# A two-layer graph kernel: the stage between its layers takes its rows in source order and shares PSUM with the second layer

## The chip, the cores and the metric

One core of a Trainium2 chip. The metric is the time of one execution on the device in microseconds (us). The engines are TensorE (PE; its weight loads are listed as PEld), VectorE (DVE), ScalarE (ACT), GpSimd (POOL) and SyncE (SP, which here only issues DMA transfers). SBUF is the on-chip memory of 128 partitions. PSUM is the matrix engine's output memory; the kernel allots it in eight banks of 2 KB a partition, each of which holds one 128 x 512 tile of f32.

## The reference

`x` is 4096 x 512, `adj` is 4096 x 4096, all f32. `adj` has about 1.6% entries that are not zero, and the whole diagonal. Layer 0 is attention with one head whose logits get the matrix added twice; layer 1 has eight heads of 64.

```
# layer 0
h = relu(layernorm(x))
q, k, v = h @ Wq.T + bq, h @ Wk.T + bk, h @ Wv.T + bv
x = x + softmax(q @ k.T * scale + adj + adj) @ v
# layer 1
h   = relu(layernorm(x))
nX  = (h @ W) as heads, (8, 4096, 64)
nX  = a_ln * (nX - mean) / (std(nX, ddof=1) + 1e-6) + b_ln
at1, at2 = nX . a1, nX . a2                      # per head and row
kg  = leaky_relu(at1 + at2.T, 0.2) * adj
att = softmax(where(adj != 0, kg, -32768))
out = x + elu(att @ nX + nX)
```

## The kernel before

**Names.** N = 4096 rows, D = 512. A block is 128 rows (P), NB = 32 of them; a chunk is SB = 4 blocks, 512 rows (GC), NI = NS = 8 of them. R = 32. HD = 64 is a head, HG = 4 heads make a head group. `seq(...)` keeps an engine's instructions in the order in which the program issues them, DMA queues included; so the order of the Python calls is the order on each engine, and instructions of different engines are held together by semaphores alone.

**Layer 0** (the loop at L742) goes over 8 chunks of 512 query rows by 32 tiles of 128 keys, two tiles at a time. PE makes logits (L585) and weighted values (L636), both as seven products for eight. At a chunk's end `chunk_end` (L671) puts the products M1 to M7 together on DVE and ACT (`ends`, L694), `total_of_rows` (L710) sums the softmax totals on PE, `divide` (L680) scales four blocks on ACT and adds `x` by an accumulating DMA from POOL's queue, and `normalize_rows` (L271) makes the layernorm of the new rows and stores it to `xn_d`, and the new rows to `x1_d`. Along the way `for_layer_1` stores the transposed matrix for layer 1: `gT_d` in f32 and a mask `nT_d` in bf16. The pool `early` holds the tiles that read the matrix (`ag`). The last chunk's `ends`, totals and divide come after the loop.

**Source order.** In layer 1 a tile of 128 sources takes rows p = 32q + r from block q of a chunk, so that tile c of a chunk has partition 32q + r hold row 128q + 32c + r. In layer 0 and in the stage before the change a block is 128 rows in their own order; `rows_of_sources` (L106) and `sources_of_rows` (L110) are views that change from one order to the other in a DMA.

**The stage between the layers** (L1073 to L1273) is a loop over blocks r. `load_normalized` loads a chunk of `xn_d` (1 MB) to `xns`. `turn(r)` transposes a block on PE (four 128 x 128) and takes relu on ACT. `project(r)` is 16 products 128 x 264 with the centred weights, to `y` in PSUM (two banks), the last 16 columns being the head sums with a1 and a2. `variance(r)` is a square on ACT, a sum by heads on DVE, and a maximum and a power -1/2 on POOL. `standardize(r)` refines the root in five small DVE operations, multiplies `y` by it to `feat` (which sets y free) and to `at`, and POOL multiplies a_ln to `own`. Once a chunk, `split` makes on DVE (14 operations) the three bf16 pieces of at1 and at2; `sides` turns them on PE for each block, copies on ACT and stores to `z1_d` and `z2_d`; `fours` does the same for `u4_d`. `store_features` writes `feat` to `nX_d`, `store_rows` writes `own` to `own_d`, and `load_targets` brings -4 times at2 (stored to `at2_d`) back in source order. `at_block(r, f)` puts a step behind block r; what is left after the loop runs in the first steps of layer 1 (`at_step`, `later`). PSUM has its own pool here: `turned` 1 bank, `y` three times 2, `side` 1. It is closed before layer 1 opens one of the same size.

**Layer 1** (from L1285) is 512 steps (8 chunks of target rows by 2 head groups by 32 source tiles); 32 steps make a group. In a step PE forms the logits of four heads (`left_sums` L888 for the next step, `sums` L878 and L908), ACT and DVE take relu and leaky, DVE and POOL multiply by the matrix `g` (L935, L932), ACT takes exp (L939), and PE multiplies by the features `nX` (L951) of four steps before, in accumulators that live for a group. Every four steps `load_adj` issues `z2`, `nb`, two `nx` and `g` (1 MB) on SP, and in the first group `load_features` issues four loads of 256 KB of `nX_d`, which go to `nX` in SBUF, in source order, for the rest of the kernel. `finish` ends a group: `copies` of the two accumulators by ACT and DVE, `to_rows` transposes on PE, `divide`, own_d added by POOL's queue (step +5), `negative` (+8), `positive`, exp, a sum (+12), x1_d added (+15), and `close` (+21) writes out.

```
        for r in range(-1, NB + 1):
            if r + 1 < NB:
                turn(r + 1)
            if 0 <= r < NB:
                project(r)
            if r >= 1:
                standardize(r - 1)
            if 0 <= r < NB:
                variance(r)
            for f in at_blocks.pop(r, []):
                f()
```

Of the kernel before, what the change touches and what calls it, by code (L numbers as in the profile page):

```python
# [79 lines left out]
def fast_path(  # L80
# [64 lines left out]
    x1_d = dram.tile([NI, 2, P, 2, SB, P], F32, name="x1_d")  # L145
# [10 lines left out]
    nX_d = dram.tile([NB, P, D], F32, name="nX_d")  # L156
    own_d = dram.tile([NI, 2, P, 2, SB, P], F32, name="own_d")
    u4_d = dram.tile([NB, NH, P], F32, name="u4_d")
    at2_d = dram.tile([NB, P, NH], F32, name="at2_d")

    def store_rows(ap, ic, rows, n):
        seq(nc.sync.dma_start(out=ap[ic, n // 2, :, n % 2], in_=rows[:, :, ts(n, P)]))
# [147 lines left out]
    with tc.tile_pool(name="early", bufs=2) as early, tc.tile_pool(name="kv", bufs=1) as kv:  # L310
# [17 lines left out]
        def load_adj0(s):  # L328

            ic, jt = TILES[s]  # L330
            ag = early.tile([P, GC // R, P], F32, name="ag", tag="ag", bufs=2)
            load_blocks(ag, adj[ts(ic, GC), ts(jt // SB, GC)])
            for c in range(SB):
                raws[s + c] = ag
# [44 lines left out]
        with tc.tile_pool(name="proj_c", bufs=1) as pc, tc.tile_pool(  # L379
# [10 lines left out]
            def load_x(sb):  # L390
                xt = early.tile([P, SB, D], F32, name="xt", tag="ag", bufs=2)
                for b in range(SB):
                    seq(nc.sync.dma_start(out=xt[:, b, :], in_=x[ts(sb * SB + b, P), :]))
                return xt
# [154 lines left out]
        with tc.tile_pool(name="attn", bufs=2) as work, tc.tile_pool(  # L549
# [121 lines left out]
            def chunk_end(s, ic):  # L671
# [19 lines left out]
                def then(*pairs):  # L691
                    return lambda: [seq(f(*a)) for f, *a in pairs]

                ends.extend([  # L694
                    then((copy, c11, m[1])),
# [14 lines left out]
            def total_of_rows(ic):  # L710
# [9 lines left out]
                rows_of[ic] = work.tile([P, SB], F32, name="rinv", tag="rinv", bufs=2)  # L720
# [21 lines left out]
            for s in range(0, n_tiles, 2):  # L742
# [31 lines left out]
                if jt == 0 and ic:  # L774
                    total_of_rows(ic - 1)
                weighted(s, (3, 0), (3, 1), (6, 0), (6, 1))
# [12 lines left out]
            total_of_rows(NI - 1)  # L789
            while ends:  # L790
                end()
            rests[0]()
# [5 lines left out]
    with tc.tile_pool(name="ga_g", bufs=2) as adjs, tc.tile_pool(  # L798
# [3 lines left out]
    ) as work, ExitStack() as banks:  # L802
        psum = banks.enter_context(tc.tile_pool(name="stage_ps", bufs=2, space=PSUM))
# [60 lines left out]
        def pair_rows(ap, ic, hg):  # L864

            r, c = cols(ic, hg)
            return [
                ap[r, c.start + f * P : c.start + (f + 1) * P].rearrange("(b p) d -> p b d", p=P)
                for f in range(2)
            ]  # L870
# [70 lines left out]
        def values(n, hf):  # L941
# [3 lines left out]
            if jt == 0 and hf == 0:  # L945
                grp["acc"] = [
                    psum.tile([P, GC], F32, name=f"acc{hf}", tag=f"acc{hf}", bufs=1) for hf in range(2)
                ]
            t = logits.pop(n) if hf else logits[n]
            for e in range(2):  # L950
                seq(nc.tensor.matmul(  # L951
                    grp["acc"][hf][ts(e, HD), :], nX[jt // SB][:, jt % SB, hg * HG + 2 * hf + e, :],
                    t[:, hf + 2 * e, :], start=jt == 0, stop=jt == NB - 1,
                ))

        def finish(n, ic, hg):
# [3 lines left out]
            y = work.tile([P, 2, SB * 2, HD], F32, name="y", tag="y", bufs=1)  # L960

            def room():
                grp["e"] = work.tile([P, 2, SB * 2, HD], F32, name="e", tag="ob", bufs=1)

            def copies():
                seq(nc.scalar.copy(ob[:, 0, :], grp["acc"][0]))
                seq(nc.vector.tensor_copy(ob[:, 1, :], grp["acc"][1]))

            def to_rows(hf, ks=range(2)):
# [12 lines left out]
                grp["pt"] = pt[:, :, 0 : 4 * HB].rearrange("p k (q c) -> p k q c", c=HB)  # L982

            def divide(hf, ks=range(2)):
                v = grp.pop("pt")
                rinv = inverses[:, ic, hg, hf, ks[0] : ks[-1] + 1]
                seq(nc.vector.reciprocal(rinv, v[:, :, :, HD]))  # L987
                seq(nc.vector.tensor_mul(  # L988
                    y[:, hf].rearrange("p (k q) e -> p k q e", k=2)[:, ks[0] : ks[-1] + 1],
                    v[:, :, :, 0:HD],  # L990
                    rinv.unsqueeze(3).to_broadcast([P, len(ks), 4, HD]),
                ))

            def add(t, what):
                seq(nc.gpsimd.dma_start(out=flat(t), in_=what, accum_op=ALU.add))

            def of_group(ap):
                return ap[ic, hg].rearrange("p f b d -> p (f b d)")

            def flat(t):  # L1000
                return t.rearrange("p f q e -> p (f q e)")
# [10 lines left out]
            def close():  # L1012
                e = grp["e"]
                for f, ap in enumerate(pair_rows(out, ic, hg)):
                    nc.sync.dma_start(
                        out=ap, in_=e[:, f].rearrange("p (b h) e -> p b (h e)", h=2)
                    )

            if n > n_steps:

                of_rows = [last_in[0][:, 2 * k : 2 * k + 2, :] for k in range(2)]

                def half(t, hf):
                    return t[:, hf].rearrange("p q e -> p (q e)")
# [8 lines left out]
                for hf in range(2):  # L1033
                    seq(nc.vector.tensor_add(half(y, hf), half(y, hf), of_rows[0][:, hf]))
# [3 lines left out]
                for hf, queue in enumerate((nc.sync, nc.scalar)):  # L1038
                    seq(nc.vector.tensor_add(half(e, hf), half(e, hf), half(y, hf)))
                    seq(nc.vector.tensor_add(half(e, hf), half(e, hf), of_rows[1][:, hf]))  # L1040
                    queue.dma_start(
                        out=pair_rows(out, ic, hg)[hf],
                        in_=e[:, hf].rearrange("p (b h) e -> p b (h e)", h=2),
                    )
# [6 lines left out]
            for d, f in (  # L1051
                (5, lambda: add(y, of_group(own_d))), (8, room), (8, negative), (9, positive),
                (10, lambda: exp_of(flat(grp["e"]))), (12, lambda: add(grp["e"], flat(y))),
                (15, lambda: add(grp["e"], of_group(x1_d))), (21, close),
# [3 lines left out]

        def load_features(k):
            nX.append(gat.tile([P, SB, NH, HD], F32, name=f"nX{k}"))  # L1060
            for q in range(SB):
                seq(nc.sync.dma_start(
                    out=nX[k][q * R : (q + 1) * R].rearrange("p c h e -> p c (h e)"),
                    in_=nX_d[k * SB + q].rearrange("(c r) d -> r c d", r=R),
                ))
# [10 lines left out]
        xns, feats, owns, states, ys, deviating = {}, {}, {}, {}, {}, {}  # L1076
# [6 lines left out]
        def load_normalized(ic):  # L1083
# [4 lines left out]
            seq(nc.sync.dma_start(out=xns[ic], in_=by_blocks(xn_d, ic)))  # L1088

        def turn(r):  # L1090
            m = psum.tile([P, GC], F32, name="turned", tag="turned", bufs=1)
# [4 lines left out]
        def project(r):  # L1096
            ys[r] = psum.tile([P, 2, GC], F32, name="y", tag="y", bufs=3)
            for g in range(2):
                for k in range(KC):
                    seq(nc.tensor.matmul(  # L1100
                        ys[r][:, g, 0:HW], h1s[:, r % 2, ts(k, P)], w1_sb[:, k, g, :],
                        start=k == 0, stop=k == KC - 1,
                    ))
# [14 lines left out]
        def standardize(r):  # L1118
# [9 lines left out]
            if b == 0:  # L1128
                feats[ic], owns[ic] = chunk_tile("feat"), chunk_tile("own")
                states[ic] = prep.tile([P, SB, 2, NH], F32, name="at", tag="at", bufs=2)  # L1130
            f, o = feats[ic][:, b, :], owns[ic][:, b, :]
# [16 lines left out]
        def split(ic):  # L1148

            at = states.pop(ic)  # L1150
            seq(nc.vector.tensor_add(
                at, at, at_b.unsqueeze(1).to_broadcast([P, SB, 2, NH])
            ))
            at2s = prep.tile([P, SB, NH], F32, name="at2s", tag="at2s", bufs=2)
            seq(nc.vector.tensor_scalar_mul(at2s, at[:, :, 1, :], -4.0))
            rows = slice(ic * SB, (ic + 1) * SB)
            def store_targets():
                seq(nc.sync.dma_start(out=at2_d[rows].rearrange("q p h -> p q h"), in_=at2s))

            if ic + 1 < NI:  # L1160
                at_block(SB * ic + 5, store_targets)
            else:
                at_step(2, store_targets)
            at1s = prep.tile([P, SB, NH], F32, name="at1s", tag="at1s", bufs=2)
            seq(nc.vector.tensor_scalar_mul(at1s, at[:, :, 0, :], 4.0))
            at2c = prep.tile([P, SB, NH], F32, name="at2c", tag="at2c", bufs=1)
            seq(nc.vector.tensor_mul(
                at2c, at[:, :, 1, :], coef.rearrange("p b g f e -> p b (g f e)")
            ))
            for e, (kind, first) in enumerate(((2, 3), (0, 0))):  # L1170
                rest = prep.tile([P, SB, NH], F32, name="rest", tag="rest", bufs=2)
                left = at2c if e else at[:, :, 0, :]
                for i in range(3):
                    piece = parts[:, :, kind : kind + 2, :, first + i]
                    seq(nc.vector.tensor_copy(piece, left.rearrange("p b (g h) -> p b g h", h=HG)))
                    if i < 2:
                        seq(nc.vector.tensor_sub(
                            rest.rearrange("p b (g h) -> p b g h", h=HG),
                            left.rearrange("p b (g h) -> p b g h", h=HG), piece,
                        ))  # L1180
                        left = rest
            at1ss[ic] = at1s

        def one_bank(tag):
            return banks_now[0].tile([P, GC], F32, name="m", tag=tag, bufs=1)

        banks_now = [psum]

        def sides(ic, b, tag="side"):
# [573 lines left out]
```

## Time and profile before

| what | value |
| --- | --- |
| median of three runs (lowest, highest) | 3669.55 us (3669.5, 3675.35) |
| the profiled execution: its own time, its span | 3669.51 us, 3667.7 us |
| mean granted clock of PE | 0.988 |
| busy: PE, DVE, ACT, POOL | 97%, 69%, 48%, 62% |
| first transpose of the stage (L1093) | 1846.28 us |
| first product of layer 1 (L888) | 2029.72 us |
| first group of layer 1 ends, 32 steps later | 2151.94 us |
| a step of layer 1 in its steady part | 2.968 us |

The span is the time from the first to the last instruction; 1.8 us of the execution lie around it. The rows that follow further down come from these views: the page's 40 slices (a digit is the busy share of a slice of 91.7 us in tenths); the waits (engine, line, what was waited for, total us, times, the longest); the timeline (start, length, engine, line, operation, tiles with their shapes, count, and in brackets the idle time ahead with what ended it); windows (length, then busy time and instructions of PE, PEld, DVE, ACT and POOL, the granted clock, the DMA engines' share, GB/s); and the chain of waits (start, length, what the end of the kernel depended on then).

### The profile page before, as it was taken

To read this page: it belongs to the slowest core of one execution; us is meant where nothing else is said; L and a number is where in the kernel's file an instruction comes from. 1 tells how busy PE (TensorE), PEld (TensorE's weight loads), DVE (VectorE), ACT (ScalarE), POOL (GpSimd) and SP (SyncE) were. 2 spreads that over 40 slices of the span, in tenths; PEclk is the share of its full clock that TensorE was granted. 3 is DMA by queue.
4 is the path that set the end of the run, shared out by engine and by line. 5 is a ranking of instruction groups with operands and counts; after the bars stand their busy time and mean duration, and the time that the engine had idled before them with its cause. 6 is when DMAs were issued, how large, how long until landed. Compare 5 with 4: busy or idle time off the path is not lost. (4 is left out here: it accounts for less than half of the span.)

```text
span 3667.7 us, 58811 instructions
## 1 busy us (share of the span) xinstructions
PE 3546.0 (97%) x21482; PEld 2085.7 (57%) x21482; DVE 2536.0 (69%) x4163; ACT 1746.5 (48%) x1541; POOL 2269.8 (62%) x1802
## 2 busy tenths in 40 slices
PE   8999999999999999999988789999999999999998
PEld 4447888888888888888866223222222222222232
DVE  5435565656566666656555678888888888888887
ACT  1000011111111111111133679999999899999997
POOL 4653444444444444444455568788887787888886
PEclk9999999999999999999999899999999999999999
DMA  6566788888888787888658987788877777777875
GB/s 213 181 210 207 234 240 246 231 247 242 244 235 243 242 249 243 229 256 235 199 146 212 220 206 208 205 216 212 215 205 207 197 200 210 206 211 216 210 210 151
DMA packets 667531, 796.85 MB, mean 217 GB/s; under 512 B 86817, under 2 KB 489697, under 8 KB 658017
## 3 DMA queue, kind: packets, MB, share of 16 engines
q1 hardware_dynamic: 655136, 759.64, 71.7%
q0 software_dynamic: 10704, 31.98, 5.0%
q8 instruction: 171, 2.80, 0.3%
q10 hardware_dynamic: 1392, 1.38, 0.2%
q14 instruction: 128, 1.04, 0.1%
HBM read 602.28 MB, written 182.71 MB: 214 GB/s over the span
## 5 line engine op out<-in xcount | busy, mean ns | idle before, releaser
L932 POOL TENSOR_TENSOR t<-t,g 128x1024 f32<-128x1024 f32 x512 | 1223.8, 2402 | 316.8 <-DVE t L926 226.7
L951 PE MATMUL acc<-t,nX 128*64 128x512 f32 x4096 | 1009.1, 609 | 0.0
L939 ACT ACTIVATE t<-t 128x2048 f32<-128x2048 f32 (+1 forms) x527 | 976.6, 1853 | 0.2 <-POOL t L932 0.2
L926 DVE SCALAR_TENSOR_TENSOR t<-u,at2m,r 128x512 f32<-128x512 f32 x1024 | 719.2, 744 | 205.6 <-issue 150.0
L597 ACT ACTIVATE aT<-aT 128x512 f32<-128x512 f32 x256 | 161.2, 630 | 1405.5 <-DVE aT L593 1405.5
L593 DVE TENSOR_TENSOR aT<-aT,XZ 128x256 f32<-128x256 f32 x893 | 352.3, 418 | 584.9 <-PE XZ L585 580.3
L935 DVE TENSOR_TENSOR t<-l,g 128x1024 f32<-128x1024 f32 x512 | 623.4, 1218 | 27.8 <-DMA g<-gT_d 24.7
L894 ACT ACTIVATE l<-l 128x1024 f32<-128x1024 f32 x512 | 516.4, 1009 | 155.4 <-PE l L888 108.2
L951 PEld LDWEIGHTS acc<-t,nX 128*64 128x64 f32 x4096 | 247.7, 136 | 456.7 <-issue 448.9
L585 PE MATMUL XZ<-qt,hS 128*128 128x256 f32 x2040 | 483.8, 380 | 1.9 <-DVE aT L593 1.0
L585 PEld LDWEIGHTS XZ<-qt,hS 128*128 128x128 f32 x2040 | 387.5, 190 | 57.8 <-DVE aT L593 5.1
L609 POOL TENSOR_TENSOR S<-aT 128x256 f32<-128x256 f32 x128 | 93.2, 728 | 519.8 <-ACT aT L597 519.8
L585 PE MATMUL XZ<-qt,hT 128*128 128x256 f32 x1532 | 372.5, 379 | 0.5 <-DVE aT L593 0.5
L621 POOL TENSOR_TENSOR total<-total,aT 128x256 f32<-128x256 f32 x360 | 323.2, 911 | 9.4
L585 PEld LDWEIGHTS XZ<-qt,hT 128*128 128x128 f32 x1532 | 291.0, 190 | 40.4 <-DVE aT L593 0.9
L878 PEld LDWEIGHTS <-z 6*128 6x128 bf16 x2048 | 52.3, 91 | 428.3 <-DVE t L926 344.8
L610 POOL TENSOR_TENSOR aT<-aT 128x256 f32<-128x256 f32 x128 | 93.2, 728 | 285.4 <-ACT aT L597 285.4
L636 PE MATMUL M<-v,aT 128*128 128x256 f32 x1024 | 262.8, 379 | 0.0
L636 PE MATMUL M<-tv,aT 128*128 128x256 f32 x1024 | 262.6, 379 | 0.0
L636 PE MATMUL M<-v,S 128*128 128x256 f32 x1024 | 242.5, 380 | 0.0
L888 PE MATMUL l<-z_left,z 64*64 64x512 bf16 x2048 | 203.1, 383 | 34.4 <-DVE t L935 20.9
L577 DVE SCALAR_TENSOR_TENSOR gs<-ng,aT 128x512 f32<-128x512 bf16 x256 | 225.8, 882 | 8.8
(188 smaller groups left out, 4383.8 us busy)
## 6 DMA issues: line engine op xcount, KB each, us to landing
g<-gT_d SPq DMA_DIRECT2D x128, 1024.0 KB
ag<-in_adj_dram SPq DMA_DIRECT2D x256, 256.0 KB
hS<-s_d SPq DMA_DIRECT2D x64, 1024.0 KB
gT_d<-gs SPq DMA_DIRECT2D x256, 256.0 KB
nb<-nT_d SPq DMA_DIRECT2D x128, 512.0 KB
nx<-nT_d SPq DMA_DIRECT2D x256, 256.0 KB
hT<-h_d SPq DMA_DIRECT2D x64, 768.0 KB
tv<-vt_d SPq DMA_DIRECT2D x128, 384.0 KB
```

What stands on the lines that cost most here:

```text
L577: seq(nc.vector.scalar_tensor_tensor(gs, ng, G_MASKED / NEG_BIG, aT, ALU.mult, ALU.add))
L585: seq(nc.tensor.matmul(out, a, b, start=start and k == 0, stop=k == 1, skip_group_check=not start,))
L593: seq(nc.vector.tensor_add(p, p, part))
L621: seq(nc.gpsimd.tensor_add(t, t, a))
L636: seq(nc.tensor.matmul(sums[ic][i][:, u, :], a[:, ts(u, P)], b, start=jt == 0 and u == 0, stop=jt == NB - 2, skip_group_check=u == 1,))
L888: seq(nc.tensor.matmul(lefts[n][ts(c, HD), r, :], loads[n // JB][2][ts(r, HD), jt % JB * P + c * HD :][:, :HD], groups[ic, hg]["z1_left"][ ...
L894: seq(nc.scalar.activation(lefts[n], lefts[n], AF.Relu, scale=4.0))
L926: seq(nc.vector.scalar_tensor_tensor(t[:, 2 + e, :], u4[:, e, :], at2m[:, jt, h : h + 1], right[e], ALU.max, ALU.add))
L932: seq(nc.gpsimd.tensor_mul(t[:, 2:4, :], t[:, 2:4, :], both_heads(n)))
L935: seq(nc.vector.tensor_mul(logits[n][:, 0:2, :], lefts.pop(n), both_heads(n)))
L939: seq(nc.scalar.activation(t, t, AF.Exp))
L951: seq(nc.tensor.matmul(grp["acc"][hf][ts(e, HD), :], nX[jt // SB][:, jt % SB, hg * HG + 2 * hf + e, :], t[:, hf + 2 * e, :], start=jt == 0 ...
```

## The change

1. `load_normalized` loads each chunk as four transfers of 32 partitions, in source order. `standardize` then writes the features at once to `nX` in SBUF, and `split` writes `at2m`. `nX_d`, `at2_d` and their stores and loads are gone. The stores of `z1_d`, `z2_d`, `u4_d` and `own` change order on the way (`own_d` by four transfers of 32 partitions a chunk). `ones_in` stands in the stage.
2. `variance(r)` is issued ahead of `standardize(r - 1)`.
3. One PSUM pool serves the stage and layer 1. The accumulators are one tile `accs` of two banks, for the whole pool; `y` is that tile for every third block and an `l` tile otherwise; `turn` uses r0 (the first r1), `sides` and `fours` r1.
4. `split` stays behind block 4 of the next chunk; `sides` and `fours` come two to three blocks later, some of them inside a projection. Those of the last chunk, its split in eight parts of two operations, and the last `standardize`, stand in layer 1's first 18 steps.
5. At the end of layer 0 the last chunk's additions are grouped anew (two copies on ACT), the totals stand before the last eight products, the divide comes after block 0, and the `ag` tiles have a pool of their own, so that `xns` can be loaded before layer 0 has ended.
6. `x1_d`, `own_d`, `y` and `e` have another layout: `close` is one transfer with runs of 1 KB instead of two with runs of 512 B; the addition of own_d has runs of 1 KB for 4 KB.

```diff
-    x1_d = dram.tile([NI, 2, P, 2, SB, P], F32, name="x1_d")
+    x1_d = dram.tile([NI, 2, P, SB, 2, P], F32, name="x1_d")
...
+                ] if ic + 1 == NI else [
...
+                if not more:
+                    end()
+                    total_of_rows(ic)
                 weighted(s, (3, 0), (3, 1), (6, 0), (6, 1))
...
-            total_of_rows(NI - 1)
-            while ends:
-                end()
-            rests[0]()
...
-        psum = banks.enter_context(tc.tile_pool(name="stage_ps", bufs=2, space=PSUM))
+        accs = psum.tile([P, 2, GC], F32, name="accs", tag="accs", bufs=1)
...
-                seq(nc.scalar.copy(ob[:, 0, :], grp["acc"][0]))
-                seq(nc.vector.tensor_copy(ob[:, 1, :], grp["acc"][1]))
+                seq(nc.scalar.copy(ob[:, 0, :], accs[:, 0, :]))
+                seq(nc.vector.tensor_copy(ob[:, 1, :], accs[:, 1, :]))
...
-                for f, ap in enumerate(pair_rows(out, ic, hg)):
-                    nc.sync.dma_start(
-                        out=ap, in_=e[:, f].rearrange("p (b h) e -> p b (h e)", h=2)
-                    )
+                nc.sync.dma_start(
+                    out=rows_out(ic, hg), in_=grp["e"].rearrange("p b f h e -> p b (f h e)")
+                )
...
-            seq(nc.sync.dma_start(out=xns[ic], in_=by_blocks(xn_d, ic)))
+            for q in range(SB):
+                seq(nc.sync.dma_start(
+                    out=xns[ic][ts(q, R)],
+                    in_=xn_d[ic * SB + q].rearrange("(c r) d -> r c d", r=R),
+                ))
...
-            m = psum.tile([P, GC], F32, name="turned", tag="turned", bufs=1)
+            m = one_bank("r0" if r else "r1")
...
-            ys[r] = psum.tile([P, 2, GC], F32, name="y", tag="y", bufs=3)
+            if r % 3 == 1:
+                ys[r] = accs
+            else:
+                ys[r] = psum.tile([P, 2, GC], F32, name="y", tag="l", bufs=2)
...
-            f, o = feats[ic][:, b, :], owns[ic][:, b, :]
+            f, o = nX[ic][:, b].rearrange("p h e -> p (h e)"), owns[ic][:, b, :]
...
+        def store_own(ic, q):
+            seq(nc.sync.dma_start(
+                out=own_d[ic].rearrange("(c r) b g f d -> b r c (g f d)", r=R)[q],
+                in_=owns[ic][ts(q, R)],
+            ))
...
+            places = (k + 6, k + 7, (k + 8, 3), k + 8) if ic + 2 < NI else (
+                k + 6, (k + 7, 2), (k + 7, 5), k + 7)
...
+        for ic in range(NI - 1):
+            at_block(SB * ic + 4, split_all, ic)
...
-        for r in range(-1, NB + 1):
+        for r in range(-1, NB):
             if r + 1 < NB:
                 turn(r + 1)
-            if 0 <= r < NB:
+            if r >= 0:
                 project(r)
+                variance(r)
             if r >= 1:
                 standardize(r - 1)
-            if 0 <= r < NB:
-                variance(r)
...
+        later[0, "mid"] = [lambda: standardize(NB - 1)]
...
+        def split_last():
+            pieces = split(NI - 1)
+            for n in range(2, 10):
+                later.setdefault((n, "end"), []).append(lambda: some_of(pieces, 2))
...
-            if n % JB == (2 if q == NS - 1 else 0) and q < n_steps // JB:
+            if n % JB == 0 and q < n_steps // JB:
                 load_adj(q)
-                if q < NS:
-                    load_features(q)
```

## The prediction

> **What bounds it.** First the page's 40 slices (91.7 us each), then windows, waits and chain at the stage between the layers.
>
> ```profile
> PE   8999999999999999999988789999999999999998
> DMA  6566788888888787888658987788877777777875
> ```
>
> TensorE dips only in slices 20 to 23, 1834 to 2201 us. Before them a window of 140 us of layer 0 has PE 140 us busy; after them a step of layer 1 takes 2.968 us and a group of 32 steps 98.0 (32 x 2.968 = 95.0, and some 3 of output products). So only the stage (first transpose 1846.28, first product of layer 1 2029.72: 183.4 us, 5.73 a block) and what follows it have time to give. Waits of that stretch (total, times, longest):
>
> ```profile
> ACT sqs L1107 <- PE y L1100: 94.3, 32, 4.6
> DVE nq L1123 <- POOL pw L1116: 67.7, 26, 2.8
> POOL own L1143 <- DVE at L1138: 63.9, 31, 4.0
> ```
>
> DVE waits for POOL and POOL for DVE, while PE has about 40 us of waits. The timeline of DVE shows the loop:
>
> ```profile
> 1904.11 0.17 DVE L1123 TENSOR_TENSOR nq<-pw,var 128x8 f32<-128x8 f32 x1 [0.19 <-POOL pw L1116]
> ...
> 1905.85 0.68 DVE L1114 TENSOR_REDUCE var<-sqs 128x8 f32<-128x512 f32 x1
> 1909.31 0.17 DVE L1123 TENSOR_TENSOR nq<-pw,var 128x8 f32<-128x8 f32 x1 [2.79 <-POOL pw L1116]
> ...
> 1914.58 0.17 DVE L1123 TENSOR_TENSOR nq<-pw,var 128x8 f32<-128x8 f32 x1 [2.79 <-POOL pw L1116]
> ```
>
> Standardize (1.8 us), then on POOL own 1.27, max 0.25, power 1.67, then standardize again: 5.27 a block. Split adds 3.4 a chunk on DVE, so a chunk takes 21.5, of which the windows show PE (first pair, then the next four engines) at work:
>
> ```profile
> 1926.00:1947.00 21.00, 17.23 (x97) 14.35 (x95) 11.50 (x44) 6.78 (x13) 12.75 (x12) 1.00 0.92 255
> 1969.00:1990.00 21.00, 17.36 (x97) 14.48 (x97) 11.48 (x43) 6.78 (x13) 12.75 (x12) 1.00 0.92 227
> ```
>
> Group 0 of layer 1 (2029.72 to 2151.94, 122.2 us against 98) is late by DMA; its chain:
>
> ```profile
> 2085.61 10.65 DMA nX<-nX_d
> ...
> 2096.33 15.55 DMA g<-gT_d
> ...
> 2130.15 9.36 DMA nx<-nT_d
> ...
> 2146.97 11.96 DMA g<-gT_d
> ```
>
> **Start of the stage.** It begins so:
>
> ```profile
> 1841.98 0.95 PE L717 MATMUL XZ<-ones,total 128*128 128x1 f32 x8
> ...
> 1846.28 1.09 PE L1093 MATMUL turned<-ident,xns 128*128 128x128 f32 x4 [3.35 <-DMA xns<-xn_d]
> ...
> 1849.11 1.12 PE L1093 MATMUL turned<-ident,xns 128*128 128x128 f32 x4 [1.74 <-ACT h1s L1094]
> ```
>
> Loading xns early takes its 3.35 us away, but the shared PSUM pool makes the first transpose wait for DVE's last addition of layer 0. The totals' products now stand ahead of the last eight (1.89 us), and POOL's totals still end at 1841.94: PE ends at 1841.98 + 0.19 + 1.89 = 1844.1, the last additions (four of about 0.62) near 1846.5. First transpose 1846.6, so nothing gained. The divide (four ACT operations, 2.56 us) no longer stands before the first relu: 1846.6 + 1.1 + 1.1 and the projection of 5.05 (slow after the pause, as in the trace; 3.78 later) end near 1853.5 against 1855.1. **-1.6.** Divide after block 0 lies in ACT's slack (1.8 of 4 us a block); if not, it costs up to 2.6 once.
>
> **Variance a block ahead.** The loop opens: the power has a whole block's time. What is late next? Per block DVE has 2.4, with a quarter of the split (3.4) 3.3; POOL 1.27 + 0.25 + 1.67 = 3.2; ACT 1.2 and 0.15 for sides; PE 0.22 + 3.78 = 4.00, the pitch seen at 1854.90 to 1870.90, before the loop had filled up. PE is last. Its cost: 31 x 4.00 = 124.0, 28 sides at the pitch 0.22 each 6.2, 7 fours at 0.25 1.8: 1853.5 + 132 = 1985.5. Split stands on DVE ahead of a standardize that frees a y buffer. There are three of these, as before, so 4 us of lead cover its 3.4, and nothing is late unless the row statistics of the last chunk (two pairs, 1.6 us on DVE; 3.1 on POOL at 1897.6) meet it: 1.6 once. Some 1.5 for the banks that turn and sides change between. First product of layer 1 near **1988.6 against 2029.7: -41.1.** Sides moved two to three blocks later cover PE's 13.3 and 9.1 us of waits for standardize and split; without that cover these 22 us come back. Chunk 7's standardize leaves the boundary (5.5 us of PE's wait) for step 0.
>
> **DMA taken away.** nX_d (8 stores, 8 x 4 loads, 16 MB), at2_d (8 stores, 32 loads), two z transfers in other directions (same bytes). Added: xns in four issues for one, 24 more on SP's queue, against 72 fewer; own_d still four a chunk. SP is free in the stage; the twelve early xns issues pass x1_d's stores, which group 0 reads first at step 15 of its end; in group 0 SP's queue loses 28 loads before g. ones_in's memset (0.09, eight times) moves along on DVE.
>
> Against it speaks a rule of the Trainium skill (SBUF — State Buffer, "Door 1: The DMA port swizzle" with the setup-cost knee): a transfer over 32 partitions reaches half of the ports, 189 GB/s at 1 MiB against 328 over all, so one large one is better. By row, nX's loads had this very form, 10.65 us for the last one landing, in a queue with others. By the rule, an estimate: own and xns 5.5 us a chunk each, 11 of 17; by the row, two such megabytes are at worst 21, past the chunk. I take the rule's 11, since the row is of a loaded queue and xns is asked for more than a chunk ahead: cost 0; upper end 4 us a chunk, 24 in all.
>
> **Group 0.** Steady 95.0. Steps 0 and 1: relu behind sqs, zc and the last standardize (1.8 on DVE), 2.9. Split of chunk 7, formerly in one piece (step 3 took 6.96), in eight steps of two operations: about 0.2 each, 1.5. Sides and fours on ACT, five times 0.48, 2.2. DMA: 2.13 MB a quad for 3.13; in 12 us that is 180 GB/s, where later groups carry 208 without stalls. Windows of a late and a steady stretch (DMA share, GB/s last):
>
> ```profile
> 2090.00:2120.00 30.00, 24.32 (x170) 6.74 (x168) 17.94 (x24) 19.67 (x15) 16.57 (x7) 0.89 1.09 235
> 2300.00:2340.00 40.00, 40.00 (x328) 11.56 (x330) 34.02 (x42) 38.58 (x29) 35.09 (x17) 1.00 0.89 215
> ```
>
> I leave 2 for own_d's last stores: 95 + 2.9 + 1.5 + 2.2 + 2 = **104 against 122.2: -18.6**, bounds 99 and 118. Group 1's first two steps (4.14 and 4.24) inherit a late g: -2.
>
> **Groups' ends.** The accumulators become one tile of two banks. The trace before:
>
> ```profile
> 2564.77 0.58 ACT L966 COPY ob<-acc 128x512 f32<-128x512 f32 x1
> ...
> 2565.01 0.68 DVE L967 COPY ob<-acc 128x512 f32<-128x512 f32 x1
> ```
>
> These overlap; in the new program DVE's waits for ACT's, ACT's for both halves' products, and behind DVE's stand the next step's leaky and PE's next values. A rule of the Trainium skill (PSUM — Partial Sum Buffer, "PSUM bank collisions raise a hardware error") asks to guard by bank and quadrant; the two are different banks, so by rule they may run side by side and the sum is 0. The program's tile decides: DVE starts 0.35 later; x 15 = **+5.5** (0 to 10). Tail: ACT later by 0.7, and four more small divides 0.6: **+1.5**. close() as one transfer instead of two: the stalls at step 29, 17 us over all groups, come from loads queued behind it on SP; I take 5 of them away, between 0 and 10: **-5.** own_d's accumulate on POOL's queue comes in 512 runs of 1 KB, not 128 of 4 KB: issue 0.87 to at most 1.36 (the row of x's, 512 runs), landing 5.5 to 10.4 (the same row); negative comes three steps, 8.9 us, later. It is nearest to x's row in runs but has half of its bytes: 7, no wait. Upper end: 1.5 x 15.
>
> **Sum.** -1.6 - 39.5 (together the 41.1) - 18.6 - 2 + 5.5 + 1.5 - 5 = -60 off the span of 3667.7 gives 3607.7; with 1.8 around the span **3609.5**. The profiled run (3669.51) is at the median of the runs (3669.55).
>
> **Rivals.**
> - *DVE bounds the stage* (17 in 100). Split and reduce stand in one queue with the standardize that frees y: 3.3 busy of 4.0 is no wide margin, and each semaphore hop costs. At 4.6 a block the stage ends 0.6 x 31 = 19 later: 3628. Against it: DVE's gaps between dependent small operations are 0.03.
> - *The stream of adjacency is itself late in group 0* (17 in 100): four chain pieces are two g, one nx, only one nX; z and u4 stores and the first loads have to wait for each other on SP. Then two thirds of the 18.6 stay: 3622. Against it: share 1.09 there, against 0.89.
> - *The shared PSUM undoes the overlap; slower* (4 in 100). One mechanism: a projection waits for a standardize of its y (accs or l), and turn for sides' copy in r1. If PE's product, sqs, reduce, power and standardize of a block became a chain (3.8 + 0.6 + 0.7 + 1.9 + 1.8 = 8.8), 32 x (8.8 - 5.73) = +98 in the stage, -20 after it: 3747. It decides from a pitch of 5.73 + 20/32 = 6.35. Against: three y buffers are given, which put two blocks between.
> - *The first overlap is absent* (it already is in my sum: transpose waits for additions). If it works, 3 us less.
> - *Stage better still, and step-29 stalls go* (10 in 100): 3596.
>
> **Numbers.** Likeliest 3609.5 (52 in 100), own range 3600 to 3619. Together with the rivals 3594 to 3632. What can be told from no change is 0.2%, 7.3 us. Faster 0.95, same 0.01 (a third of the stage's gain, none of group 0's), slower 0.04.
>
> **What would show it.** Right: turned every 4.0 us, no nq wait on pw, PE windows above 0.95 busy in the stage; left_sums near 1989; group 0 near 104 with no step over 5; copies of accs one after the other. Wrong: turned waiting for at or for zc, y waiting for DVE; g still in the chain of group 0; negative waiting for own_d.

## The result and the profile after

| | before | changed kernel | forecast |
| --- | --- | --- | --- |
| median | 3669.73 us (3669.5 to 3675.35, 4 runs) | 3612.3 us (3609.13 to 3612.49, 4 runs) | 3609.5 us (3594 to 3632) |
| span of the profiled execution | 3667.7 | 3610.4 | 3607.7 |
| first transpose of the stage | 1846.28 | 1846.87 | 1846.6 |
| first product of layer 1 | 2029.72 | 1991.73 | 1988.6 |
| group 0 of layer 1 | 122.2 | 108.4 | 104 |

Times and spans are in us. The ratio of the times is 0.9838, with a 95% interval from 0.9821 to 0.9855. In the 40 slices of the changed kernel the dip of PE has shrunk from four digits to one, the 23rd slice (1986 to 2076 us), and DMA there and in the next slice has fallen from 9 and 8 to 6 and 6:

```profile
PE   8998999999999999999999899999999999999998
...
DMA  7567788888878888888858668877878877787885
```

The waits of PE in the stage, first before (1850 to 2030 us, 35 us in all) and then in the changed kernel (1850 to 1992 us, 4 us in all):

```profile
PE m L1193 <- DVE nq L1123: 13.3, 5, 3.3
PE m L1193 <- DVE parts L1175: 9.1, 2, 5.3
```

```profile
PE accs L1103 <- DVE at L1144: 3.1, 3, 2.1
PE m L1205 <- ACT zc L1210: 0.6, 1, 0.6
PE y L1103 <- DVE at L1144: 0.5, 3, 0.2
```

PE's wait for split is gone, and in the view of all engines (1843 to 2000 us) so is DVE's wait for POOL's power. In its place stands this row:

```profile
POOL pw L1120 <- DVE nq L1128: 32.6, 22, 4.3
```

POOL now waits for DVE to come to the next block, which is idle time that nobody pays for. The windows of two stretches in the stage (PE is the first pair) show PE 96% and 99% busy, where it had been 82% and 83% in the two windows of before that the prediction shows, and DVE at 15.5 to 17.2 of 21 to 22:

```profile
1926.00:1947.00 21.00, 20.22 (x111) 16.79 (x110) 15.48 (x56) 6.98 (x14) 15.19 (x15) 1.00 1.00 240
1947.00:1969.00 22.00, 21.82 (x125) 18.38 (x124) 17.20 (x67) 8.20 (x16) 14.28 (x15) 1.00 0.85 179
```

The windows of the whole stage, before and changed, show one thing more:

```profile
1846.28:2029.72 183.44, 146.83 (x759) 121.68 (x760) 97.18 (x369) 56.87 (x107) 104.75 (x105) 0.94 0.69 179
1846.87:1991.73 144.86, 140.67 (x759) 117.68 (x759) 98.66 (x360) 55.49 (x105) 100.05 (x101) 0.98 0.73 158
```

Of the 38.6 us between them 32.4 are idle time of PE. The other 6.2 are busy time for the same number of products, while the granted clock rose from 0.94 to 0.98. No run here separates the clock from the waits.

In group 0 the windows (the same columns; the last two are the share of the DMA engines and GB/s) show that the transfers no longer fill the engines. The chain of that stretch has one piece of DMA of 3.0 us and one of 2.0 in place of the four of 9 to 16, and DVE's rows have no gap beside either of the two:

```profile
1992.00:2100.00 108.00, 95.21 (x745) 27.17 (x745) 95.26 (x123) 87.19 (x69) 76.57 (x35) 0.92 0.68 190
```

```profile
1996.77 3.01 DMA nb<-nT_d
...
2006.67 2.04 DMA z<-z_d
```

By its steps (counted by their first products) the first 13 of group 0 went from 48.8 to 50.2 us and the other 19 from 73.4 to 58.2, in which PE is now busy all the time. The windows of these 19, before and changed:

```profile
2078.50:2151.94 73.44, 62.94 (x462) 17.76 (x454) 48.49 (x62) 53.70 (x39) 44.77 (x20) 0.93 1.00 215
2041.94:2100.15 58.21, 58.21 (x477) 16.51 (x469) 48.23 (x57) 55.41 (x43) 45.01 (x20) 1.00 0.74 207
```

The span's 57.3 us come from: the time up to layer 1's first product, -38.0; group 0, -13.8; everything from there to the last step's first product, 1488.1 to 1481.3, -6.8; the tail behind it, 27.65 to 29.0, +1.3.

### The profile page after: what moved, and what is told of

The parts are those of the page before. It is cut to its first block, busy times and chain, and to the rows that moved or that the text cites. A ratio compares the mean times of both kernels' runs of the same rounds, so it can differ in the third digit from the quotient of the medians.

```text
span 3610.4 us, 58670 instructions
## 1 busy us (share of the span) xinstructions
PE 3528.8 (98%) x21482; PEld 2078.8 (58%) x21482; DVE 2550.9 (71%) x4167; ACT 1745.5 (48%) x1542; POOL 2272.5 (63%) x1802
## 4 chain that ended last, share of the span: by engine, by line
PE 86%; DVE 8%; DMA 3%; ACT 1%; issue 1%; SPq 0%; POOL 0%; DVEq 0%; ACTq 0%; POOLq 0%
PE accs L950 23%; PE XZ L585 20%; PE M L636 20%; PE r L911 4%; PE r L881 4%; PE l L891 3%; PE pq L461 3%; PE l L911 2%; PE pv L435 2%; DVE t L938 2%; PE y L1103 1%; DMA nx<-nT_d 1%; PE pt L976 1%; DVE y L989 1%; DVE x L692 1%
## 5 line engine op out<-in xcount | busy, mean ns | idle before, releaser
L950 PE MATMUL accs<-t,nX 128*64 128x512 f32 x4096 | 1003.1, 605 | 4.7 <-DVE ob L966 4.7
L597 ACT ACTIVATE aT<-aT 128x512 f32<-128x512 f32 x256 | 161.2, 630 | 1403.7 <-DVE aT L593 1403.7
L950 PEld LDWEIGHTS accs<-t,nX 128*64 128x64 f32 x4096 | 246.5, 136 | 460.3 <-issue 447.9
```

What stands on the lines that cost most here:

```text
L950: seq(nc.tensor.matmul(accs[ts(e, HD), hf, :], nX[jt // SB][:, jt % SB, hg * HG + 2 * hf + e, :], t[:, hf + 2 * e, :], start=jt == 0, stop ...
```

## The experiments

A single run is not read to the microsecond. Some groups have a long step, most often step 29 of 32, and which of them have it differs from run to run of the same program: repeated, the changed kernel had groups 3 and 11 of 104.2 and 103.6 us where the first profile shows 98.4 and 100.5, and a median of 3613.93 us (3608.49 to 3622.82, five runs). The runs were also made on several chips, on which the median of the kernel before was 3663.7 to 3673.3 us. So the stage (first transpose to first product of layer 1), group 0 and the normal group (one without a long step) are compared, and the time only beside them. All but the first two rows, the repeated one, best1 and best3 are single runs:

| run | stage | group 0 | normal group | time |
| --- | --- | --- | --- | --- |
| before | 183.4 | 122.2 | 98.0 | 3669.5 |
| changed | 144.9 | 108.4 | 98.4 | 3612.3 |
| changed, repeated | 145.2 | 108.7 | 98.4 | 3613.9 |
| order_back | 168.9 | 112.8 | 98.4 | 3644.0 |
| before_ahead | 180.0 | 121.1 | 98.0 | 3668.6 |
| sides_early | 161.2 | 108.4 | 98.4 | 3631.0 |
| before_both | 166.7 | 120.9 | 98.0 | 3651.7 |
| reload | 155.0 | 130.3 | 98.4 | 3644.9 |
| split_whole | 144.5 | 106.3 | 98.4 | 3612.7 |
| split_pool | 143.4 | 102.6 | 98.4 | 3612.0 |
| acc_apart | 145.2 | 108.6 | 98.0 | 3608.9 |
| best1 | 145.2 | 102.5 | 98.0 | 3606.1 |
| best3 | 145.1 | 102.0 | 98.0 | 3599.3 |

**The order of variance and standardize.** First it was put back in the changed kernel (order_back), then made alone in the kernel before (before_ahead):

```diff
                 project(r)
-                variance(r)
             if r >= 1:
                 standardize(r - 1)
+            if r >= 0:
+                variance(r)
```

> The changed kernel with variance(r) put back behind standardize(r - 1), everything else as changed. Theory (the order is what opened the loop between DVE and POOL): a block returns to 5.27 us plus the split's 3.4 a chunk, 21.5 us a chunk against some 17.5, so the first product of layer 1 comes 25 to 35 us later than 1991.7 and the time is 3637 to 3647. Rival (the other parts carry the stage's gain: sides placed later, xns early, banks shared): the stage ends within 8 us of the changed kernel's, time at most 3620.

> The kernel before with only variance(r) moved ahead of standardize(r - 1). Theory of the prediction (PE's 22 us of waits for standardize and split at the early sides come back when only the order is changed): the stage shortens by 15 to 20 of the 38 us, time 3650 to 3655. Rival (those waits were only the loop's lateness, and go with it): the stage shortens by 30 or more, time 3640 or less. In both, group 0 of layer 1 stays near 122 us.

Put back, the stage grew by 24.0 us, just under the theory's 25 to 35, and the time by 31.7. The loop of DVE and POOL is there again (the waits view of order_back, 1850 to 2008 us), and PE waits 21.3 us for the standardize that sets y free (PE's view of the whole stage):

```profile
DVE nq L1128 <- POOL pw L1121: 59.4, 23, 2.8
```

```profile
PE y L1103 <- DVE at L1144: 12.3, 15, 1.6
PE accs L1103 <- DVE at L1144: 9.0, 9, 2.4
```

Made alone it brought 3.4 us, far less than either theory said. The loop is gone there, but PE waits for the other engines at another place (the waits view of before_ahead, 1850 to 2008 us):

```profile
PE m L1193 <- DVE parts L1175: 18.3, 6, 3.2
...
PE m L1208 <- ACT zc L1198: 5.6, 6, 0.9
```

PE stands at the first sides of each chunk until split is done, up to 3.2 us each; over the whole stage these are seven waits and 21.3 us, where before had 22.4. So the order is needed and is not enough.

**The places of the sides.** The text ahead of the result and the prediction call the new places two to three blocks later. By the two programs the sides moved by one block at most: with chunks 0 to 5, whose first block is k, they stood behind blocks k+5, k+6, k+7 and k+8, and stand behind k+6 and k+7, within k+8 and behind k+8. In the changed kernel they were put back (sides_early), and in the kernel before the order and later places were made together (before_both):

```diff
-            places = (k + 6, k + 7, (k + 8, 3), k + 8) if ic + 2 < NI else (
+            places = (k + 5, k + 6, k + 7, k + 8) if ic + 2 < NI else (
```

```diff
-                    at_block(r + 1 + b, sides, ic, b)
+                    at_block(r + min(2 + b, 4), sides, ic, b)
```

> The changed kernel with the sides of chunks 0 to 5 at blocks k+5, k+6, k+7, k+8 instead of k+6, k+7, within k+8, k+8. Theory of the prediction (the later places cover PE's waits for split): 6 chunks x 3 us, stage up by 15 to 20, time 3628 to 3632. Rival (with variance ahead, split's results are there in time, and the early places cost only a part of a split's 3.4 us or nothing): stage up by 0 to 6, time 3612 to 3618.

> The kernel before with variance(r) ahead of standardize(r - 1) and the sides one block later (behind blocks k+6, k+7, k+8, k+8), nothing else of the change. Theory (order and places are each other's condition: with both, DVE's split of 3.4 us and its standardize have a block to finish before PE asks for them): the 18.3 us of PE's waits for split go, the stage shortens by 20 to 28 us of the 38, time 3644 to 3652. Rival (the shared banks, the sources kept in SBUF and the emptier queue are needed too): the stage shortens by less than 12, time 3658 or more.

sides_early: the stage is 16.3 us longer, and the wait is the one that was named (its waits view):

```profile
PE m L1205 <- DVE parts L1187: 14.7, 6, 2.8
```

before_both: 16.7 us shorter than before, under the theory's 20 and over the rival's 12. The wait for split has gone, but two sides behind one block and fours beside them share one PSUM bank, and PE waits for ACT to copy it. The waits view of before_both shows these, and PE's at the stage's end:

```profile
PE m L1208 <- ACT zc L1198: 9.8, 7, 2.7
PE m L1193 <- ACT zc L1198: 6.3, 7, 0.9
...
PE l L888 <- issue: 3.3, 1, 3.3
```

Of the 21.8 us that its stage is still longer than the changed kernel's, these three rows make 19.4. In the changed kernel one sides and most fours stand inside a projection, so that ACT's copy lies beside products (0.6 us of such waits), and the last standardize has gone to step 0. That these two are most of the rest of the gain is read from the waits; no run made them alone.

**The features that stay in SBUF.** In reload they are stored and loaded again, at the places, sizes and runs of before:

```diff
+            at_block(k + 6, store_features, ic)
...
+                if q < NS:
+                    load_features(q)
```

> The changed kernel, with the features also stored to DRAM (1 MB a chunk) and loaded again into the same tiles in the first group, at the places, sizes and runs of the kernel before; the values are the same. Theory (the transfers of nX are what made group 0 late): group 0 goes from 108.4 to 120 to 128 us, the whole time up by 12 to 20, to 3624 to 3632. Rival (the stalls of group 0 belonged to the stream of the matrix itself and to the split of the last chunk): group 0 stays under 113 us, time at most 3617.

Group 0 grew by 21.9 us to 130.3, over the 120 to 128 expected, and the stage by 10.1, which the theory had not counted (its chain waits 7.5 us for xns and three times 4.5 to 6.5 for z there); so the time, 3644.9, is over the 3624 to 3632 too. In group 0 the chain of reload has the pieces of before again, the matrix's own loads among them, and its window is full:

```profile
2027.16 14.55 DMA nX<-nX_d
...
2041.81 16.22 DMA g<-gT_d
```

```profile
1999.00:2126.00 127.00, 102.84 (x721) 28.30 (x720) 92.75 (x121) 84.75 (x66) 74.67 (x34) 0.87 1.02 229
```

So the late loads of g were late because of nX: the rival that gave them to the matrix's stream alone falls. And the transfers were worth more than group 0's net gain of 13.8, since the same change put something else there: 15.2 by the last 19 steps, 21.9 by this run.

**What that something is.** The timeline of the changed kernel in a step of group 0, two rows of DVE and then the row of POOL:

```profile
2014.72 1.48 DVE L1187 CAST parts<-at 128x32 bf16<-128x32 f32 x1
...
2016.24 0.21 DVE L1190 TENSOR_TENSOR rest<-at,parts 128x32 f32<-128x32 f32 x1
```

```profile
2013.74 2.37 POOL L935 TENSOR_TENSOR t<-t,g 128x1024 f32<-128x1024 f32 x1 [1.54 <-DVE t L929]
```

The cast takes 0.23 us elsewhere. Here it ends at 2016.20, just after POOL's multiplication, which ends at 2016.11; the operation behind it is short. The first of each of split's seven pairs shows this (1.44 to 1.63 us), so steps 4 to 10 take 3.6 to 4.2 us for 2.97. Two runs tested it: all 14 operations at once (split_whole), and all of them on POOL (split_pool):

```diff
-            for n in range(2, 10):
-                later.setdefault((n, "end"), []).append(lambda: some_of(pieces, 2))
+            later.setdefault((2, "end"), []).append(lambda: some_of(pieces, 14))
```

```diff
-            pieces = split(NI - 1)
+            pieces = split(NI - 1, nc.gpsimd)
```

> The changed kernel with the split of chunk 7 in one piece at the end of step 2, not two operations at the end of steps 2 to 9. Theory (the first small DVE operation of each pair has to wait until POOL's multiplication of 2.35 us is over, for about 1.3 us, eight times): in one piece it waits once, 1.3 + 3.2 us in one step, so group 0 goes from 108.4 to 103 to 105 us and the time to 3607 to 3609. Rival (DVE's busy time is what is paid, it has only 0.3 us a step to spare): the same 14 operations cost the same or more in one piece, group 0 at 108 to 110.

> The changed kernel with the 14 operations of chunk 7's split on POOL, still two at the end of steps 2 to 9. Theory (what is paid in these steps is DVE waiting for POOL, not the operations): POOL has 0.57 us to spare in a step of 2.97, two of its small operations take 0.4 to 0.6, so steps 4 to 11 fall from 3.8 to 4.2 to about 3.0 to 3.3 and group 0 to 99 to 102 us, time 3603 to 3606. Rival (the steps are long because of DMA or of ACT, not of DVE): group 0 at 107 or more.

In one piece DVE waits once (its first operation 1.52 us, the other 13 about 0.2) and two steps are long, 5.77 and 5.45; group 0 fell by 2.1, less than the 3 to 5 expected, as the second step is late too. On POOL an operation takes 0.25 to 0.33 us, group 0 fell by 5.8 to 102.6, just short of the 99 to 102 expected, and steps 4 to 10 lie at 2.97 but for two. POOL had the time, and what DVE paid was the wait. The total of both runs stayed at the changed kernel's and so missed what was expected, since long steps near other groups' ends (groups of 104.7 and 104.2 us) took the gain back.

**The accumulators.** acc_apart has two tiles again, in a pool opened when the stage's `accs` has been read:

```diff
-                seq(nc.scalar.copy(ob[:, 0, :], accs[:, 0, :]))
-                seq(nc.vector.tensor_copy(ob[:, 1, :], accs[:, 1, :]))
+                seq(nc.scalar.copy(ob[:, 0, :], grp["acc"][0]))
+                seq(nc.vector.tensor_copy(ob[:, 1, :], grp["acc"][1]))
```

> The changed kernel with two accumulator tiles for layer 1, as before the change, in a PSUM pool that is opened when the stage's accs has been read. Theory (the one tile of two banks makes DVE's copy wait for ACT's): each normal group goes from 98.4 to 98.0 us, 15 times 0.4 = 6, the tail from 29.0 to about 28, time 3605 to 3606. Rival (the 0.4 comes from the runs of 1 KB or the other layout of y): groups stay at 98.4, time 3612.

The two copies at a group's end, in the changed kernel and then in acc_apart (timeline):

```profile
2510.19 0.58 ACT L965 COPY ob<-accs 128x512 f32<-128x512 f32 x1
2510.80 0.69 DVE L966 COPY ob<-accs 128x512 f32<-128x512 f32 x1 [0.29 <-ACT ob L965]
```

```profile
2310.11 0.58 ACT L976 COPY ob<-acc 128x512 f32<-128x512 f32 x1
2310.35 0.68 DVE L977 COPY ob<-acc 128x512 f32<-128x512 f32 x1
```

Side by side again, and a normal group is 98.0 us: the 0.4 of each group is the shared tile's, not the new layout's. The time, 3608.9 for 3605 to 3606, has one group of 104.4 in it.

**Together.** best1 joins split_pool and acc_apart; best3 also puts the last standardize ahead of step 0's leaky:

```diff
-        later[0, "mid"] = [lambda: standardize(NB - 1)]
+        at_step(0, standardize, NB - 1)
```

> split_pool and acc_apart together. If each cost stands by itself the gains add: 7 to 9 and 6 to 7 us, time 3597 to 3600. If the end of group 0 hides one of them, 3602 to 3606.

> The changed kernel itself, beside the next one on the same chip: 3609 to 3613.

> The changed kernel with chunk 7's split on POOL, two accumulator tiles, and the last standardize ahead of step 0's leaky instead of behind it (so that its small DVE operations run before POOL's first multiplication, not beside it: one of them took 2.27 us there). Theory: the wait of 3.42 us at step 2 shrinks to about 1 to 2, group 0 from 102.5 to 100 to 102, and with the other two the time is 10 to 14 us under the changed kernel's. Rival (DVE's chain at the start of layer 1 is only moved ahead, and leaky of step 0 is late by as much): group 0 stays at 102 to 103, 10 to 12 us under.

best1: 3606.06 us (3598.91 to 3610.88), ratio 0.9836 (0.9801 to 0.9872). Its profiled run has both local gains, 102.5 and 98.0, and long steps in four groups. The median misses the 3597 to 3600 of gains that add, and its ratio can't be told from the change's 0.9838. best3, beside the changed kernel on one chip: 3599.29 us (3597.73 to 3609.2) against 3613.93 (3608.49 to 3622.82); ratios to before 0.9827 (0.9799 to 0.9854) and 0.9856 (0.9828 to 0.9884). These intervals overlap, so the 15 us between the medians aren't shown to be all its own; the stage times say 6.7 for group 0 and 0.4 for each group. The standardize put ahead brought 0.5 of the 6.40 at step 1, not the 1.4 to 2.4 expected. best3's timeline shows why: its first operation ran beside another multiplication of POOL, the `own` of the block before, and was held by that one:

```profile
1996.23 1.22 DVE L1139 TENSOR_TENSOR nq<-pw,var 128x8 f32<-128x8 f32 x1 [0.30 <-POOL pw L1132]
```

```profile
1996.16 1.26 POOL L1160 TENSOR_TENSOR own<-nX,aln_sb 128x512 f32<-128x512 f32 x1
```

The rest of the stall is DVE's queue: from 1993.43 to 2000.48, when leaky ends that PE waits for, it has no gap over 0.11 us but the one of 0.30.

## Why the prediction was right, point by point

- **The bound.** PE is last in the stage, as said: the pitch of 4.00 is there from 1854.60 to 1870.60, chunks behind the third take 17.1 to 18.3 us, and the rival that DVE would hold it at 4.6 falls. The first product of layer 1 came 38.0 us earlier, not 41.1: the first projection ended 1 us later than put (it took 5.99 for 5.05, at a granted clock of 0.63), and the block with the last chunk's statistics took 6.72 (2.5 over its 4.22 where I had 1.6). Small waits for y and the banks (2.1 us where 1.5 was put) make a part of the rest. One step of the working was wrong without harm: four blocks of 5.27 and 3.4 for split are 24.5, not 21.5. The chunk did take 21.5, because the block with split in it took 5.8 for 5.27: most of split ran while DVE waited for POOL anyway.
- **Which part carries it.** The prediction put the gain on the order and said of the later sides that without them 22 us come back. sides_early brought back 16.3. But the order alone was worth 3.4 and not the 15 to 20 that I then expected of it: each of the two hides the other's effect.
- **The first overlap** is absent, as the sum had it: DVE's last additions of layer 0 end at 1846.66, where 1846.5 was put, and the first transpose starts at 1846.87.
- **Group 0** gave -13.8 for -18.6, and the sign "no step over 5" did not come: step 1 took 6.40, though steps 0 and 1 together cost 3.5 where 2.9 was put. The mechanism of the transfers was right, and the 2 us left for DMA were not needed. The failed term is "in eight steps of two operations: about 0.2 each, 1.5": the 14 operations fill seven steps, and these hold 7.3 us over 2.97. I added up operations on DVE and did not ask what POOL was doing beside them, though the trace of before has the very row: the first operation of the last chunk's split took 1.46 us beside the same multiplication of POOL (2037.41, 2.35 us), where the next one took 0.18:

```profile
2038.38 1.46 DVE L1151 TENSOR_TENSOR at<-at,at_b 128x64 f32<-128x64 f32 x1
```

- **The rule against this change** (the Trainium skill, SBUF — State Buffer, "Door 1: The DMA port swizzle": a transfer over 32 partitions reaches half of the ports): cost 0 was taken, at most 24. DMA was 1.00 busy in the window 1926 to 1947, and PE lost under 1 us there; if the transfers were as long as the rule has them, they were covered. No run here measures one of them by itself.
- **The groups' ends.** +5.5 for the copies was 15 times 0.4 = 6; the tail +1.5 was +1.3. own_d's accumulate landed after 5.8 us (issue 1.21) where 7 was put. Group 1's first two steps fell from 4.15 and 4.24 to 2.97 each, 2.4 where 2 was put. The 5 us from close() at step 29 are not confirmed: what is left of the -6.8 behind group 0 is about 10 us in the first profile, but the long steps move between runs of one program, so one profile can't say what is due to close().
- **The slower side** (PSUM shared between the stage's steps) shows as 4 us of PE's waits in the stage, against the 20 us that it would have needed.
- **The closeness of the total** is in part luck. The stage and group 0 gave 7.9 us less than put, and the groups' ends 5.5 more, almost all of it from the long steps that move from run to run. The mechanisms of the two large terms are shown by the runs above; that the sum came within 3 us is not.

## What to carry to other kernels

When two waits stand in one loop, removing one may show little: undo each in the good version as well as making each in the old one, and read what is waited for instead. Price an operation that is moved beside another engine by the rows it will lie beside, not by its own length. A wait between readers of one tile can come from the tile and not from the data, so tiles that different engines read at the same time are better kept apart.

## What the runs showed of the hardware that was not expected

A small DVE operation issued while POOL multiplied two tiles of 128 x 1024 in SBUF was held until that ended: 1.48 us instead of 0.23 for a cast, 1.52 instead of about 0.2 for an addition of two small tiles, 2.27 instead of 0.19 for a multiplication of two small tiles at 1996.24. POOL's `own` (128 x 512, 1.27 us) held them too, 1.22 instead of 0.16 in best3. Beside POOL's power (1.67 us, two tiles of 128 x 8) casts ran in 0.23 and subtractions of two small tiles in 0.21, in the kernel before and in the changed one. DVE's large operations with an input in PSUM ran beside the multiplication in their usual 0.74 and 1.21. The Trainium skill states the rule (SBUF — State Buffer, "Who interferes with whom"): DVE's copies, casts and scalar operations in their fast forms, and those with two inputs in SBUF while POOL reads SBUF, contend with POOL for a shared port pair, and the second to come is blocked for the whole instruction. The rows agree with it for the multiplication and `own`; that the power did not block is not explained by it.
